# Layer norm 1 of two of four batches on a host-transposed input, in a cross-attention block on one core

## The chip, the core and the metric

The kernel runs on one NeuronCore of a Trainium2 chip. The core has a matrix engine (TensorE, PE in the profile), a vector engine (VectorE, DVE), a scalar engine for activations (ScalarE, ACT), a general engine (GpSimd, POOL) and a sync engine (SyncE, SP) that here issues nearly all DMAs. Each engine works through its own list of instructions in order, and semaphores hold an instruction back until what it needs is there. The metric is the device time of one execution in microseconds, as the median of several runs.

## The reference

Four batches; `hidden_states` x is 4 x 512 x 512, the encoder's states are 4 x 512 x 512, 16 heads of 32, an MLP of 2048, all in float32:

```python
residual = hidden_states
x = layer_norm(hidden_states, ln1_w, ln1_b)
q = (x @ q_w + q_b)          # 16 heads of 32
k = (encoder_hidden_states @ k_w + k_b)
v = (encoder_hidden_states @ v_w + v_b)
scores = jnp.einsum('bhqd,bhkd->bhqk', q, k) * scale
attn = jax.nn.softmax(jnp.where(mask, scores, mask_value), axis=-1)
out = jnp.einsum('bhqk,bhkd->bhqd', attn, v)
hidden = out @ cproj_w + cproj_b + residual
y = layer_norm(hidden, ln2_w, ln2_b)
y = jax.nn.gelu(y @ fc_w + fc_b, approximate=True)
return hidden + y @ proj_w + proj_b
```

Layer norm takes the mean and the variance over the last dimension of each row, subtracts, multiplies by the inverse deviation, and then scales and shifts each column by its weight and bias.

## The kernel before, in words

The attention is done in 16 units, `w` = 0 to 15: unit `w` is batch `b = w // 4` and a group of four heads. For each unit, three preparations run on TensorE ahead of their use: `prep_k` (tile `acck`, L218), `prep_q` (`accq`, L228) and `prep_v` (`accv`, L240). Each is sixteen or four matmuls into one PSUM tile, which ScalarE then empties (L220, L231, L245); GpSimd adds the bias of v (L252). In each unit four query tiles `qt` go through `scores` (TensorE L262, then VectorE adds the mask and finds the minimum, L266, and ScalarE takes the exponential, L270) and `turn` (VectorE transposes 32 x 32 blocks into `tb`, L285 and L293; `rsum` and `rr`, L290 and L292, are the inverse sums). Every two query tiles make one half of a unit, which is rearranged across partitions by 16 DMAs (`copies`, L328, called the exchange) into `pT`, or into parts of `gt` or `xe`. `attend` (L345) then multiplies by v, and VectorE scales into `oT` (L350). There are two buffers of `tb` and one `pT`. Where all four units of a batch are done, `cproj` (L386, L387) projects and adds the residual.

Layer norm 1 of a batch runs some units ahead. `load_x` brings x in four row tiles `xn` (tag of a pool of four buffers), `ln1` takes statistics on VectorE (`ln_stat`, L128 and L129), GpSimd takes the inverse deviation by a power (`ln_rs`, L134 and L136), and `ln_norm` normalises, on VectorE (L150) or, for the keys in `BY_ACT`, on ScalarE (L146, with one more small tile `nm` from GpSimd). `ln_turn` then transposes: for each of four chunks `d`, four 128 x 128 TensorE transpositions (L159) into one PSUM tile `tp`, which is emptied into `xT` with the column's weight and bias, on VectorE for d = 1 and 2 (L162) or on ScalarE (L164). `xT` and the transposed encoder `eT` are two parts of one tile, `xe`; `load_enc` fills `eT` from an array that the host has already transposed. `prep_q` multiplies by `xT`.

Layer norm 2 of a batch goes the same way from `h` into `yT`, with `norm2` and `ln2_turn`. The MLP of batch 0 and part of batch 1's runs between the attention units, in pairs of chunks (`fc_by_pair`, seven products instead of eight, L495, with VectorE's sums L455 and ScalarE's Gelu L513, after a table load), with weight sums on GpSimd (`fc_sums`, L452, L455). The other MLPs come at the end. All accumulations share four PSUM buffers of the pool `ps_acc`, taken in turn.

The order of the work is written out by hand. For each unit `first[w]` and `later[w]` list pieces of work, each a function with a cost. Where `first[w]` is a tuple, its four parts go behind the four query tiles; else the pieces are spread over the four tiles by their costs. A piece issues the instructions of all engines in that order. The pieces `x1`, `x2`, `x3`, `x4` of `inputs(b)` are the load of x, the three parts of `ln1`, the four of `ln1_turn`, and the load of the encoder. DMAs of `nc.sync` go to SyncE's queue in the order of the pieces. `load_w(w + 2)` inside each preparation loads the weights of two units on.

Of the kernel before, what the change touches and what calls it, by code (L numbers as in the profile page):

```python
# [24 lines left out]
NT = L // P  # L25
ND = D // P
# [12 lines left out]
IN_XE = (25, 27, 29, 31)  # L39

AT = {u: (u - 5) // 2 for u in (5, 7, 9, 11, 13, 15, 17, 19, 53, 55, 57, 59, 61, 63)}
BY_ACT = ((1, 1), (1, 2))
MW = 8
WARM = 9
PW = 2 * NT * HG * HD
# [2 lines left out]
LN1W, LN1B, QB, KB, LN2W, LN2B, FCB = 0, 4, 8, 12, 16, 20, 24  # L48
# [1 line left out]


@with_exitstack
def xattn_block(ctx: ExitStack, tc: tile.TileContext, x, encT, mask, q_w, k_w, v_w, c_w, fc_w, p_w, vecs, rows, out):
    nc = tc.nc
    scale = float(np.float32(1.0) / np.sqrt(HD).astype(np.float32))

# [74 lines left out]
    def ln_rs(key):  # L131

        ve = small.tile([P, NT], F32, tag="ve", name=f"ve{key[0]}_{key[1]}")
        nc.gpsimd.tensor_scalar(ve, S["mv", key][:, :, 1], EPS, 1.0, ALU.add, ALU.mult)  # L134
        rs = small.tile([P, NT], F32, tag="rs", name=f"rs{key[0]}_{key[1]}")
        nc.gpsimd.tensor_tensor(rs, ve, nhalf, ALU.pow)  # L136
        S["rs", key] = rs
        if key in BY_ACT:
            nm = small.tile([P, NT], F32, tag="nm", name=f"nm{key[0]}_{key[1]}")
            nc.gpsimd.tensor_tensor(nm, S["mv", key][:, :, 0], rs, ALU.mult)  # L140
            nc.gpsimd.tensor_scalar(nm, nm, -1.0, 0.0, ALU.mult, ALU.add)
            S["nm", key] = nm

    def ln_norm(key, t, dst, src):
        if key in BY_ACT:
            nc.scalar.activation(  # L146
                dst, src, AF.Identity, bias=S["nm", key][:, t : t + 1], scale=S["rs", key][:, t : t + 1]
            )
# [30 lines left out]
    def ln1(b, part):  # L179

        xn = S["xn", b]
        for t in range(NT):
            if part == 2:
                ln_norm((1, b), t, xn[t], xn[t])
            elif t // 2 == part:
                ln_stat((1, b), t, xn[t])
        if part == 1:
            ln_rs((1, b))

    def ln1_turn(b, d):  # L190
        ln_turn((1, b), d, S["xn", b], xT)
# [186 lines left out]
    def c_bias(b):  # L378
        for t in range(NT):
            add_row(S["h", b, t], 0)  # L380
# [339 lines left out]
    def do(fn):  # L720
        return [(0.0, fn)]
# [10 lines left out]
    def C(b):  # L732
        return [(CHAIN, lambda t=t: cproj(b, t)) for t in range(NT)]
# [15 lines left out]
    def inputs(b):  # L749
        ln = [(0.0, lambda part=part: ln1(b, part)) for part in range(3)]  # L750
        return do(lambda: load_x(b)), ln, turns1(b), do(lambda: load_enc(b))
# [55 lines left out]
        [(CHAIN, lambda: prep_q(1))]  # L807
    )
    first[1] = [q2] + x2[2:], [k4], [v4], [q3]
    first[2] = x3[:2] + [k5], x3[2:], [v5], [q4]  # L810
    first[3] = [q5], [k6], [v6], [q6] + do(lambda: c_bias(0))
    mlp = []
    for p in range(SPLIT):
        mlp += FC(p, 0) + FC(p, 1) + PJ(p, 0) + FC(p, 2) + PJ(p, 1) + FC(p, 3) + PJ(p, 2) + PJ(p, 3)
# [25 lines left out]
    def stat(b, *ts_):  # L840
        return do(lambda: [stat2(b, t) for t in ts_])

    def norm(b, *ts_):
        return do(lambda: [norm2(b, t) for t in ts_])


    x1, x2, x3, x4 = inputs(2)
    k, q, v = A(7)
    c, t2 = C(0), turns2(0)
    first[4] = x1 + [k, q, v] + x4  # L850
    later[4] = c[:1] + x2[:1] + c[1:2] + x2[1:2] + c[2:3] + x2[2:] + c[3:]
    k, q, v = A(8)
    first[5] = (
        [k] + stat(0, 0, 1, 2, 3) + rs(0) + do(fc_sums) + x3 + norm(0, 0, 1, 2, 3) + [v], [q] + t2 + do(lambda: y_sums(0)), some(2) + pb_(0), some(2)
    )
    k, q, v = A(9)
    x1, x2, x3, x4 = inputs(3)
    first[6] = [k, q] + some(4) + [v] + x1
    k, q, v = A(10)
    first[7] = [k, q] + x2[:1] + some(2) + x2[1:2] + some(2) + [v]  # L860

    k, q, v = A(11)
    first[8] = h_(1, 0, 1) + x2[2:] + [k, q] + x3[:2] + some(2) + x3[2:3] + [v] + x3[3:] + h_(1, 2, 3) + x4
    later[8] = cb(1) + C(1)
    k, q, v = A(12)
    first[9] = [q] + some(2) + [k] + some(2) + [v]
    k, q, v = A(13)
    first[10] = [k, q] + some(4) + [v]
    k, q, v = A(14)
# [107 lines left out]
```

## Time and profile before

| what | us |
|---|---|
| runs shown: median (lowest to highest) | 803.5 (801.28 to 803.75) |
| profiled execution, its own time | 801.93 |
| profiled execution, span of the profile | 800.2 |
| TensorE matmul records, busy | 785.3 |
| VectorE busy | 573.8 |
| ScalarE busy | 339.5 |
| GpSimd busy | 123.9 |

The profile's records hold for each instruction its start, its length and what ended the idle time before it. The page sums these by group and follows the chain of work that ended last. The records of TensorE are modelled at their ends, so busy TensorE is not TensorE at its peak. In the fences, lines of a timeline read: start, length, engine, line, operation, out<-in, shape, count, and in brackets the idle time before and its releaser. Lines of a group of instructions end in: busy us, mean ns of one, idle before. A DMA line gives KB of each and the median us from issue to landing. A line of windows gives the stretch, its length, the busy time and count of PE, PEld (weight loads), DVE, ACT and POOL, the TensorE clock granted as a share of full speed, the share of the DMA engines that was busy, and GB/s.

The parts of the trace that matter here: unit 4 runs from about 119 to 154 us, unit 5 from 154 to 194, unit 8 from 259 to 300, unit 9 from 300 to 332.

### The profile page before, as it was taken

Reading aid. Unit: us, or ns where it says so; the run is one execution under the profiler, and the core shown is the slowest. Engines: PE = TensorE matmul, PEld = TensorE weight load, DVE = VectorE, ACT = ScalarE, POOL = GpSimd, SP = SyncE. Lnnn points to the kernel's source line nnn. Section 1 sums busy time; section 2 is a strip of 40 time slices with the busy share of each in tenths; the row PEclk is TensorE's granted clock in tenths of the full one; section 3 lists DMA queues with packets and bytes.
Section 4 is the critical chain, followed back from the end, with each engine's and each line's share of the span. In section 5 each row is a group of like instructions: output and inputs, shape, how many; then the busy total and the mean of one; then the engine's idle time right before and its main releaser. Section 6 shows DMA issues by size and latency. Waiting matters only on the chain.

```text
span 800.2 us, 12085 instructions
## 1 busy us (share of the span) xinstructions
PE 785.3 (98%) x4178; PEld 499.4 (62%) x4178; DVE 573.8 (72%) x1179; ACT 339.5 (42%) x745; POOL 123.9 (15%) x146
## 2 busy tenths in 40 slices
PE   9999999989999999999999999999999999999998
PEld 6545455456655645556553433446888888888887
DVE  3789998888888857779878988546738983368511
ACT  2567765547763636456554479500201220022100
POOL 1210030055121141001220100020040020200011
PEclk9999999999999999999999999999999999999999
DMA  8889999847897777787777799882325330033001
GB/s 325 289 230 241 235 237 244 231 115 182 209 240 196 211 210 192 179 198 199 181 173 213 205 261 246 202 254 93 117 84 172 118 106 14 27 86 86 1 14 40
DMA packets 60957, 137.15 MB, mean 171 GB/s; under 512 B 12464, under 2 KB 15664, under 8 KB 60768
## 3 DMA queue, kind: packets, MB, share of 16 engines
q1 hardware_dynamic: 59472, 132.43, 61.3%
q0 software_dynamic: 896, 2.82, 1.1%
q10 hardware_dynamic: 528, 1.14, 0.7%
q8 instruction: 33, 0.54, 0.3%
q14 instruction: 28, 0.23, 0.1%
HBM read 58.22 MB, written 6.82 MB: 81 GB/s over the span
## 4 chain that ended last, share of the span: by engine, by line
PE 87%; DVE 6%; SPq 3%; ACT 1%; issue 1%; DMA 1%; POOL 0%; DVEq 0%; POOLq 0%; ACTq 0%
PE q L495 20%; PE accp L554 8%; PE sc L262 7%; PE accc L386 7%; PE av L345 7%; PE accv L240 6%; PE acck L218 6%; PE accq L228 5%; PE accf L536 3%; DVE ptt L266 3%; SPq L328 2%; PE q4p L622 2%; PE q3p L622 2%; PE q5p L622 2%; PE q6p L622 2%; PE q7p L622 2%
## 5 line engine op out<-in xcount | busy, mean ns | idle before, releaser
L270 ACT ACTIVATE ptt<-ptt,mn 128x512 f32<-128x512 f32 x256 | 181.7, 711 | 135.1 <-DVE mn L266 134.8
L266 DVE CUSTOM_DVE_ANT_0 ptt<-sc,mb 128x512 f32<-128x512 f32 x256 | 161.0, 685 | 32.7 <-PE sc L262 32.4
L285 DVE STREAM_TRANSPOSE tb<-ptt 128x1024 f32<-128x1024 f32 x96 | 119.2, 1242 | 14.4 <-ACT ptt L270 12.9
L554 PE MATMUL accp<-pbt,gt 128*128 128x512 f32 x192 | 86.7, 600 | 0.0
L495 PE MATMUL q<-yT,gt 128*128 128x256 f32 x320 | 78.9, 379 | 0.0
L262 PE MATMUL sc<-pbt 32*128 32x512 f32 x512 | 73.0, 640 | 4.7 <-DVE mn L266 2.5
L513 ACT ACTIVATE ga<-ga,vec 128x512 f32<-128x512 f32 x40 | 26.7, 714 | 93.2 <-DVE ga L455 93.2
L495 PEld LDWEIGHTS q<-yT,gt 128*128 128x128 f32 x320 | 60.8, 190 | 8.7 <-issue 0.5
L554 PEld LDWEIGHTS accp<-pbt,gt 128*128 128x128 f32 x192 | 35.2, 190 | 49.0 <-issue 46.4
L240 PEld LDWEIGHTS accv<-ptt,xe 128*128 128x128 f32 x512 | 58.7, 192 | 9.5 <-issue 6.7
L495 PE MATMUL q<-ys,gt 128*128 128x256 f32 x240 | 61.8, 380 | 0.5 <-DVE ys L452 0.5
L240 PE MATMUL accv<-ptt,xe 128*128 128x128 f32 x512 | 60.8, 277 | 0.0
L218 PE MATMUL acck<-xe,ptt 128*128 128x512 f32 x128 | 59.1, 605 | 0.0
L228 PE MATMUL accq<-xe,ptt 128*128 128x512 f32 x128 | 58.4, 599 | 0.0
L386 PE MATMUL accc<-wc,oT 128*128 128x512 f32 x128 | 56.6, 596 | 0.0
L495 PEld LDWEIGHTS q<-ys,gt 128*128 128x128 f32 x240 | 45.4, 190 | 7.4 <-DVE ys L452 0.9
L345 PE MATMUL av<-pT,v 128*32 128x256 f32 x768 | 48.1, 392 | 1.8 <-DMA gt<-tb 0.7
L498 ACT COPY p<-q 128x256 f32<-128x256 f32 x28 | 9.9, 355 | 92.5 <-PE q L495 92.5
L270 ACT ACTIVATION_READ_ACCUMULATOR ptt<-ptt,mn 128x1 f32 x256 | 47.8, 187 | 0.0
L252 POOL TENSOR_TENSOR v<-v,row 128x512 f32<-128x512 f32 x16 | 20.4, 1275 | 172.9 <-ACT v L245 172.8
L228 PEld LDWEIGHTS accq<-xe,ptt 128*128 128x128 f32 x128 | 23.6, 190 | 32.4 <-issue 30.4
L262 PEld LDWEIGHTS sc<-pbt 32*128 32x128 f32 x512 | 20.0, 182 | 37.9 <-issue 21.4
(137 smaller groups left out, 1071.4 us busy)
## 6 DMA issues: line engine op xcount, KB each, us to landing
pT<-tb SPq DMA_DIRECT2D x384, 136.0 KB, 2.4
pbt<-p_w_dram SPq DMA_DIRECT2D x40, 256.0 KB, 3.1
gt<-fc_w_dram SPq DMA_DIRECT2D x40, 256.0 KB, 2.6
gt<-tb SPq DMA_DIRECT2D x64, 136.0 KB, 3.4
xe<-tb SPq DMA_DIRECT2D x56, 136.0 KB, 3.1
pbt<-fc_w_dram SPq DMA_DIRECT2D x24, 256.0 KB, 3.9
ptt<-k_w_dram SPq DMA_DIRECT2D x16, 256.0 KB, 3.8
xe<-encT_dram SPq DMA_DIRECT2D x16, 256.0 KB, 4.6
```

Of the source, the lines that this page charges most:

```text
L218: nc.tensor.matmul(acc, S["wk", w][:, d, :], eT[:, d, :], start=(d == 0), stop=(d == ND - 1))
L228: nc.tensor.matmul(acc, S["wq", w][:, d, :], xT[:, d, :], start=(d == 0), stop=(d == ND - 1))
L240: nc.tensor.matmul(acc[:, ts(t, P)], eT[:, d, ts(t, P)], S["wv", w][:, d, :], start=(d == 0), stop=(d == ND - 1),)
L262: nc.tensor.matmul(sc[:, h, :], qT[r, ts(qt, P)], kT[r, :], start=True, stop=True)
L266: nc.vector.tensor_tensor_reduce(out=s, in0=sc[:, h, :], in1=S["mb", w // NG], scale=1.0, scalar=FMAX, op0=ALU.add, op1=ALU.min, accum_out=mn,
L270: nc.scalar.activation(s, s, AF.Exp, bias=mn, scale=-1.0, accum_out=sums[:, qt, h : h + 1])
L285: nc.vector.transpose(*two_heads[k])
L345: nc.tensor.matmul(av[ts(h, HD), : 2 * P].rearrange(shape, **kw), v[:, t, ts(h, HD)], p[t][h], start=(t == 0), stop=(t == NT - 1),)
L386: nc.tensor.matmul(acc, S["oT", b][:, g, ts(t, P)], wc[:, g, :], start=(g == 0), stop=(g == NG - 1))
L495: nc.tensor.matmul(o, x[:, k], y[:, k], start=(k == 0), stop=(k == 1))
L554: nc.tensor.matmul(acc, gT[q % 2][:, k, ts(t, P)], S["pw", b, q * FQ + k], start=(k == 0), stop=(k == FQ - 1))
L622: nc.tensor.matmul(o[:, t], a[:, c, ts(t, P)], w[:, c], start=(c == pairs[0]), stop=(c == pairs[-1]))
```

## The change

The host also hands in x transposed (`xT`, in the kernel `xTd`), and batches 2 and 3 (`ROWS`) take layer norm 1 in another way. The row tiles of x are still loaded and the statistics taken from them. `ln1_rows` then makes on GpSimd a small tile `sr` with mean and inverse deviation; `store_rows` writes it to DRAM as two rows of 512; `load_rows` reads each row back, broadcast over 128 partitions, into two buffers of the pool of `xn`. `load_xT` loads the transposed x straight into `xT`; `norm_xT` subtracts and multiplies by the rows on GpSimd, eight passes of 128 x 512; `affine_xT` scales and shifts on ScalarE. The normalisation of row tiles, the transpositions and the emptying of their PSUM tiles fall away for these two batches. Batch 1's layer norm 1 stays as it was; layer norm 2 of batch 0 is now normalised on ScalarE (`NORM_ACT`), with VectorE still emptying two of its four PSUM tiles.

The lists of work change: x of batch 2 is loaded in unit 2 and its statistics are taken in unit 3 (both in unit 4 before), its rows are stored at the end of unit 3; in unit 5 the order becomes k, scale-and-shift, q, v; in unit 9 it becomes k, an MLP pair, scale-and-shift, q (q, pair, k before); in unit 8 the load of weights for v comes ahead of the exchange.

```diff
-BY_ACT = ((1, 1), (1, 2))
+BY_ACT = ((1, 1),)
+NORM_ACT = ((1, 1), (2, 0))
+ROWS = (2, 3)
...
         if part == 1:
-            ln_rs((1, b))
+            ln1_rows(b) if b in ROWS else ln_rs((1, b))
+
+    def ln1_rows(b):
+        mv = S["mv", (1, b)]
+        ve = small.tile([P, NT], F32, tag="ve", name=f"ve1_{b}")
+        nc.gpsimd.tensor_scalar(ve, mv[:, :, 1], EPS, 1.0, ALU.add, ALU.mult)
+        sr = small.tile([P, 2, NT], F32, tag="sr", bufs=1, name=f"sr_{b}")
+        nc.gpsimd.tensor_tensor(sr[:, 1], ve, nhalf, ALU.pow)
+        nc.gpsimd.tensor_scalar(sr[:, 0], mv[:, :, 0], 1.0, 0.0, ALU.mult, ALU.add)
+        S["sr", b] = sr
+
+    def store_rows(b):
+        S["dr", b] = dram.tile([2, L], F32, tag=f"dr{b}", name=f"dr{b}")
+        nc.sync.dma_start(out=S["dr", b].rearrange("s (t p) -> p s t", p=P), in_=S["sr", b])
+
+    def load_rows(b):
+        S["rw", b] = [tiles.tile([P, L], F32, tag="xn", name=f"rw{s}_{b}") for s in range(2)]
+        for s in range(2):
+            nc.sync.dma_start(out=S["rw", b][s], in_=S["dr", b][s : s + 1, :].broadcast_to([P, L]))
+
+    def load_xT(b):
+        for d in range(ND):
+            nc.sync.dma_start(out=xT[:, d, :], in_=xTd[b, ts(d, P), :])
+
+    def norm_xT(b):
+        for d in range(ND):
+            nc.gpsimd.tensor_tensor(xT[:, d, :], xT[:, d, :], S["rw", b][0], ALU.subtract)
+            nc.gpsimd.tensor_tensor(xT[:, d, :], xT[:, d, :], S["rw", b][1], ALU.mult)
+
+    def affine_xT(b):
+        for d in range(ND):
+            wd, bd = (vec[:, i + d : i + d + 1] for i in (LN1W, LN1B))
+            nc.scalar.activation(xT[:, d, :], xT[:, d, :], AF.Identity, bias=bd, scale=wd)
...
-    first[2] = x3[:2] + [k5], x3[2:], [v5], [q4]
-    first[3] = [q5], [k6], [v6], [q6] + do(lambda: c_bias(0))
+    x1, x2 = inputs(2)[:2]
+    first[2] = x3[:2] + [k5], x3[2:], [v5] + x1, [q4]
+    first[3] = [q5], [k6] + x2[:1], [v6] + x2[1:2], [q6] + do(lambda: c_bias(0)) + do(lambda: store_rows(2))
...
-    first[4] = x1 + [k, q, v] + x4
-    later[4] = c[:1] + x2[:1] + c[1:2] + x2[1:2] + c[2:3] + x2[2:] + c[3:]
+    first[4] = do(lambda: load_rows(2)) + [k, q, v] + do(lambda: load_xT(2)) + x4 + do(lambda: norm_xT(2))
+    later[4] = c
     k, q, v = A(8)
     first[5] = (
-        [k] + stat(0, 0, 1, 2, 3) + rs(0) + do(fc_sums) + x3 + norm(0, 0, 1, 2, 3) + [v], [q] + t2 + do(lambda: y_sums(0)), some(2) + pb_(0), some(2)
+        [k] + stat(0, 0, 1, 2, 3) + rs(0) + do(lambda: affine_xT(2)) + [q] + norm(0, 0, 1, 2, 3) + do(fc_sums),
+        [v] + t2 + do(lambda: y_sums(0)), some(2) + pb_(0), some(2)
     )
...
-    first[7] = [k, q] + x2[:1] + some(2) + x2[1:2] + some(2) + [v]
+    first[7] = [k, q] + x2[:1] + some(2) + x2[1:2] + some(2) + do(lambda: store_rows(3)) + [v]
...
-    first[8] = h_(1, 0, 1) + x2[2:] + [k, q] + x3[:2] + some(2) + x3[2:3] + [v] + x3[3:] + h_(1, 2, 3) + x4
-    later[8] = cb(1) + C(1)
+    first[8] = (
+        h_(1, 0, 1) + do(lambda: load_rows(3)) + [k, q] + some(2) + do(lambda: load_xT(3)) + [v] + h_(1, 2, 3) + x4
+    )
+    later[8] = cb(1) + do(lambda: norm_xT(3)) + C(1)
     k, q, v = A(12)
-    first[9] = [q] + some(2) + [k] + some(2) + [v]
+    first[9] = [k] + some(2) + do(lambda: affine_xT(3)) + [q] + some(2) + [v]
...
+        "xT": np.ascontiguousarray(a["x"].transpose(0, 2, 1)),
```

More of the change, by code (lines that the diff above doesn't have):

```diff
@@ L52, in xattn_block @@
 @with_exitstack
-def xattn_block(ctx: ExitStack, tc: tile.TileContext, x, encT, mask, q_w, k_w, v_w, c_w, fc_w, p_w, vecs, rows, out):
+def xattn_block(ctx: ExitStack, tc: tile.TileContext, x, xTd, encT, mask, q_w, k_w, v_w, c_w, fc_w, p_w, vecs, rows, out):
     nc = tc.nc
@@ L137, in ln_rs @@
         S["rs", key] = rs
-        if key in BY_ACT:
+        if key in NORM_ACT:
             nm = small.tile([P, NT], F32, tag="nm", name=f"nm{key[0]}_{key[1]}")
@@ L144, in ln_norm @@
     def ln_norm(key, t, dst, src):
-        if key in BY_ACT:
+        if key in NORM_ACT:
             nc.scalar.activation(
@@ L844, in norm @@
         return do(lambda: [norm2(b, t) for t in ts_])
-    x1, x2, x3, x4 = inputs(2)
+    x4 = inputs(2)[3]
     k, q, v = A(7)
     c, t2 = C(0), turns2(0)
-    first[4] = x1 + [k, q, v] + x4
-    later[4] = c[:1] + x2[:1] + c[1:2] + x2[1:2] + c[2:3] + x2[2:] + c[3:]
+    first[4] = do(lambda: load_rows(2)) + [k, q, v] + do(lambda: load_xT(2)) + x4 + do(lambda: norm_xT(2))
+    later[4] = c
     k, q, v = A(8)
     first[5] = (
-        [k] + stat(0, 0, 1, 2, 3) + rs(0) + do(fc_sums) + x3 + norm(0, 0, 1, 2, 3) + [v], [q] + t2 + do(lambda: y_sums(0)), some(2) + pb_(0), some(2)
+        [k] + stat(0, 0, 1, 2, 3) + rs(0) + do(lambda: affine_xT(2)) + [q] + norm(0, 0, 1, 2, 3) + do(fc_sums),
+        [v] + t2 + do(lambda: y_sums(0)), some(2) + pb_(0), some(2)
     )
     k, q, v = A(9)
-    x1, x2, x3, x4 = inputs(3)
+    x1, x2, _, x4 = inputs(3)
     first[6] = [k, q] + some(4) + [v] + x1
     k, q, v = A(10)
-    first[7] = [k, q] + x2[:1] + some(2) + x2[1:2] + some(2) + [v]
+    first[7] = [k, q] + x2[:1] + some(2) + x2[1:2] + some(2) + do(lambda: store_rows(3)) + [v]
     k, q, v = A(11)
-    first[8] = h_(1, 0, 1) + x2[2:] + [k, q] + x3[:2] + some(2) + x3[2:3] + [v] + x3[3:] + h_(1, 2, 3) + x4
-    later[8] = cb(1) + C(1)
+    first[8] = (
+        h_(1, 0, 1) + do(lambda: load_rows(3)) + [k, q] + some(2) + do(lambda: load_xT(3)) + [v] + h_(1, 2, 3) + x4
+    )
+    later[8] = cb(1) + do(lambda: norm_xT(3)) + C(1)
     k, q, v = A(12)
-    first[9] = [q] + some(2) + [k] + some(2) + [v]
+    first[9] = [k] + some(2) + do(lambda: affine_xT(3)) + [q] + some(2) + [v]
     k, q, v = A(13)
```

## The prediction

> **What bounds the kernel now.** I read the page first: busy times and the chain that ended last.
>
> ```profile
> PE 785.3 (98%) x4178; PEld 499.4 (62%) x4178; DVE 573.8 (72%) x1179; ACT 339.5 (42%) x745; POOL 123.9 (15%) x146
> PE 87%; DVE 6%; SPq 3%; ACT 1%; issue 1%; DMA 1%; POOL 0%; DVEq 0%; POOLq 0%; ACTq 0%
> ```
>
> TensorE carries 87% of the chain and its records leave some 15 us of 800 uncovered. From 192 to 435 us the chain is TensorE alone: there, work taken off it is gained in full, and any wait put in front of it is paid in full. VectorE relief is worth nothing there. Second, the chain in order of time where it leaves TensorE, in unit 5 (the first of the two places the change rewrites), with TensorE's timeline and clock (four lines of the chain: start, length, what; two of the timeline; one window).
>
> ```profile
> 171.64 0.40 ACT rr L292
> 172.04 0.59 ACT pbt L231
> 172.68 0.66 PE tp L159 x4
> 173.35 3.61 PE av L345 x32
> ...
> 168.16 1.47 PE L159 MATMUL tp<-ident,xn 128*128 128x128 f32 x12
> 172.68 0.66 PE L159 MATMUL tp<-ident,xn 128*128 128x128 f32 x4 [3.05 <-ACT pbt L231]
> ...
> 170.00:180.00 10.00, 7.30 (x53) 4.02 (x54) 8.05 (x18) 4.97 (x11) 4.91 (x4) 0.83 0.15 35
> ```
>
> Twelve transpositions of layer norm 2 of batch 0 run; the fourth group waits 3.05 us for a PSUM buffer that ScalarE empties late (L231 stands behind four exponentials, those behind VectorE). Then the clock granted is half for 3.4 us (0.83 over this window, the last column but two), and an L345 group takes 3.61 us for its usual 1.86. So this place costs 3.05 + 1.75 = 4.8 us. Third, the orders of ScalarE and TensorE in unit 9, the second place:
>
> ```profile
> 310.63 1.03 PE L495 MATMUL q<-ys,pbt 128*128 128x256 f32 x4
> 311.50 3.60 PE L218 MATMUL acck<-xe,ptt 128*128 128x512 f32 x8
> 313.62 1.33 ACT L513 ACTIVATE gt<-gt,vec 128x512 f32<-128x512 f32 x2 [2.09 <-DVE gt L455]
> 315.13 0.69 ACT L220 ACTIVATE pbt<-acck,vec 128x512 f32<-128x512 f32 x1 [0.18 <-PE acck L218]
> ```
>
> Now TensorE goes from the products of an MLP pair (L495) straight to `acck`, whose inputs lie ready, while ScalarE's Gelu waits for VectorE's sums until 313.62. Last, SyncE's queue (start, length), then the us to landing of a DMA, then prices of instructions (busy us, mean ns):
>
> ```profile
> 98.31 10.17 SPq L328 DMA_DIRECT2D gt<-tb  x16
> 133.20 1.81 SPq L177 DMA_DIRECT2D xn<-x_dram  x4
> 136.06 12.80 SPq L328 DMA_DIRECT2D pT<-tb  x16
> 149.53 1.87 SPq L172 DMA_DIRECT2D xe<-encT_dram  x4
> ...
> pT<-tb SPq DMA_DIRECT2D x384, 136.0 KB, 2.4
> xe<-encT_dram SPq DMA_DIRECT2D x16, 256.0 KB, 4.6
> vec<-vecs_dram ACTq DMA_DIRECT2D x1, 20.0 KB, 3.9
> ...
> L146 ACT ACTIVATE xn<-xn,nm,rs 128x512 f32<-128x512 f32 x8 | 5.8, 802 | 0.0
> L357 POOL TENSOR_TENSOR h<-h,row 128x512 f32<-128x512 f32 x18 | 22.4, 1276 | 9.8 <-DMA h<-x_dram 5.7 <-PE sc L262 4.1
> ```
>
> SyncE issues without a pause from 95 to 151 us (an exchange is 16 issues at 0.635 us), so what is put into it there moves all behind it.
>
> **Removed.** 32 transpositions on TensorE: 16 a batch, 4 groups of 0.44 us = 1.75 us a batch (the pieces of 0.87, 0.44 and 0.44 us in unit 8). For batch 3 that is a gain of 1.75. For batch 2 the end of unit 5 is set by a wait, so only the replay below counts. VectorE loses the normalisations of batches 0 (L150, 3.5 us) and 3 (1.9) and two L162 (1.6); in unit 8 it is covered by TensorE, worth nothing.
>
> **Moved: statistics and loads of batch 2, from unit 4 to units 2 and 3.** Four pairs of L128 and L129, 0.8 us each, now stand in VectorE's order before the scores of unit 3. By replay its reading of the last scores of unit 3 ends at 120.0 for 117.66, and TensorE's next scores start at 120.0 for 118.77: 1.2 us late. The four loads go ahead of the exchange at 98.31, making SyncE 1.9 us late; its consumer at 112.20 loses about 1 us, part of the same 1.2. Neither adds to the end by itself if unit 5 waits for something later, which it does.
>
> **Added for batch 2, the wait.** SyncE's order is now: store of the rows, two broadcast loads that wait for the store to land, two weight loads, the exchange of unit 4, a weight load, four loads of transposed x, four of the encoder. The store (1,024 pieces of 4 bytes) has no row of its kind. Nearest: 2.4 us to landing for an exchange DMA, 3.9 for the 128 short rows of `vec`. Low end 2.4; high end, if the 1.5 us above 2.4 went by pieces, 2.4 + 8 x 1.5 = 14.4. I take 4, next to `vec`, the only short-row one. Then: store at 135.1, landed 139.2, row loads and weights 2.0, exchange from 141.2 (136.06 before), 10.2 us as it has four loads before it and not seven, x loads from 152.0, the first landed at 155.5 (between 2.4 and 4.6). GpSimd's eight passes at 1.24 (the L357 row's spacing; four took 4.97) end at 165.4. Their cover, the scores and `acck(8)`, ends at about 161.4 as the encoder loads come some 4.4 us later too. From there all is serial: ScalarE's last scale-and-shift 0.8 (L146), the last quarter of `accq(8)` 0.9, its eviction 0.7, four normalisations of batch 0 now on ScalarE 2.9 (four L146 took 2.92), four exponentials 2.9, the reciprocals and `rr` 0.6, `v`'s eviction 0.6, and with it the PSUM buffer for the fourth transposition group: 174.9. One yT eviction 0.8, L345 at full clock 1.9: next scores at 177.6, before at 176.96. Cost +0.7. Queued behind ScalarE's wait are exactly those exponentials, and VectorE's transposes behind them; GpSimd's weight sums (L452, L455, 5.9 us) slide from 164.2 to 167.2, ahead of their use after 178. Floor: if the rows came early, the statistics of batch 0 (end 164.7), GpSimd's 1.9 and ScalarE's 2.9 + 2.9 + 1.2 + 0.8 + 1.9 still give 176.4, so -0.6. Ceiling: each us of the store above 4 is a us, up to +10.4 more.
>
> The Trainium skill ("DMA: Bandwidth & Descriptors", Rules for kernel authors) speaks against the store: a last dimension that isn't contiguous becomes a descriptor for each element. The same page puts about 2 us of fixed cost on a DMA; by that alone the rows land at the floor and the total would be 805.4.
>
> **Added for batch 3, the wait on TensorE.** Loads, rows and GpSimd's passes (297 to 307) are hidden: they are due at 313. `cb(1)`'s loads and the exchange of unit 8 slide 2.5 us (280.5 to 290.7, used at 296); the encoder lands by 298 for 299. But in unit 9 `accq` now follows the MLP products, and its four scale-and-shifts stand on ScalarE behind the Gelu. On the old clock: products end 311.66, Gelu ends 314.95, first scale-and-shift 315.75, `accq` 3.44: 319.2 where `acck` ended at 315.09, so +4.1, less the 1.75 of transpositions: +2.4. The idle of 4.1 us is longer than the 3.05 that halved the clock for 3.4 us above, so I add 1.7 (half of 3.4): +4.1. Bounds 0 and 1.75 for that term.
>
> The Trainium skill ("TensorE: Matmul & The Clock Gate", What's actually happening) lets the clock fall after an idle free-running window of about 3.4 us; a gap of 4.1 need not hold a whole one. By the page the drop is not sure and the total would be 805.0; the row, a gap of 3.05 that did it, decides.
>
> **Sum.** 801.93 (profiled execution; span 800.2) + 0.7 + 4.1 = 806.7. The median of the runs shown is 803.5, by which it is 808.3. I name the middle, 807.5.
>
> **Rivals.** *A, no clock drop* in unit 9: 801.93 + 0.7 + 2.4 = 805.0. For it: gaps of 1.41 and 1.63 us elsewhere dropped nothing; against it: the 3.05. *B, the store is slow* and SyncE stands still: at 9 us to landing +5, 811.7; at 14.4, 817. For it: every us on that queue between 95 and 151 moves the exchange; against: packets of 160 bytes are short in the trace (3.9 us for all). It decides from about 4 us to landing. *C, faster*: the new order dissolves the wait in unit 5, 4.8 us, which needs `v` emptied before 170, so GpSimd done by about 160.5 and the loads landed by 150.5; with A's +2.4 the time is 801.93 - 4.8 + 2.4 = 799.5, and 797 if unit 9's wait half vanishes. For it: VectorE is 3.5 us lighter there; against: the exchange ahead of the loads ended at 148.9 even before, and four normalisations now delay the exponentials. That the transpositions are not removed is excluded: the order of instructions lacks them.
>
> **How the numbers follow.** Forecast 0.50, A 0.19, B 0.17, C 0.14. 0.3% is 2.4 us, about what can be told from no change. Slower: the forecast nearly all, B, and half of A's, as 805.0 lies at the edge: 0.70. Same: the rest of A and some of the forecast, 0.16. Faster: C, 0.14. The range 801.5 to 814 leaves out most of C and the far half of B.
>
> **What would show it.** In the profile after: an idle of about 4 us on TensorE before `accq` in unit 9, ended by ScalarE's scale-and-shift, and a half clock right after; in unit 5 `accq(8)` fed in steps of 2.5 us by GpSimd, L345 back at 1.9 us; the store's time to landing (4 assumed) and SyncE's stop before the row loads; scores of unit 5's third tile about 0.7 us later. Wrong would be: `accq` of unit 9 without an idle, GpSimd's eight passes ending before 160, or GpSimd slowed far above 1.24 us a pass.

## The result and the profile after

The changed kernel takes 825.5 us, median of four runs (822.59 to 828.16), against 803.6 us of the kernel before on the same chip (four runs, 801.28 to 804.95): a ratio of 1.0275, 95% interval 1.0232 to 1.0318. The forecast was 807.5 us, with a range up to 814. The profiled execution took 824.72 us, its span is 822.9.

The page's busy times and the chain that ended last, of the changed kernel:

```profile
PE 787.8 (96%) x4146; PEld 498.6 (61%) x4146; DVE 567.6 (69%) x1169; ACT 341.1 (41%) x747; POOL 144.6 (18%) x164
...
PE 73%; DVE 9%; SPq 8%; DMA 4%; ACT 2%; issue 2%; POOL 1%; DVEq 0%; POOLq 0%; ACTq 0%
```

TensorE's work shrank by 32 matmul records and yet its busy time is 2.5 us longer (its clock is half for 20.5 us, 3.41 before), and it holds 73% of the chain for 87%. SyncE's queue and the DMAs rose from 4% to 12%, VectorE from 6% to 9%. So most of what was lost is in waits for transfers. Where, the starts of the score groups tell (L262 of the kernel before, L296 of this one; lines have moved by 34). The columns after the first are us later than before, from one profiled execution of each kernel; at 50 us, ahead of all that was changed, these are within 0.3 us of each other.

| scores of | before, us | changed kernel | store of 8 rows | no store | early passes | batch 3 alone |
|---|---|---|---|---|---|---|
| unit 4, first tile | 118.70 | +1.46 | +2.71 | +1.86 | +2.21 | -0.85 |
| unit 5, third tile | 176.90 | +10.44 | +3.30 | +0.93 | +4.10 | -1.46 |
| unit 8, first tile | 258.81 | +10.46 | +4.04 | +1.81 | +5.03 | -0.42 |
| unit 9, first tile | 299.58 | +12.90 | +2.29 | +0.06 | +3.28 | -2.17 |
| unit 9, third tile | 316.89 | +20.27 | +8.32 | +6.09 | +3.28 | -2.17 |
| unit 15, last tile | 499.68 | +22.67 | +9.80 | +8.21 | +5.48 | -1.40 |

(The last four columns belong to the experiments.) The 22.7 us of the changed kernel are 1.5 up to unit 4, 9.0 in units 4 and 5, 2.5 in units 6 to 8 (4.2 lost, since 1.75 of transpositions are saved there), 7.4 in unit 9 and 2.4 later.

**Units 4 and 5.** SyncE's queue in the timeline of the changed kernel (start, length, line, what), and its DMAs (KB of each, median us to landing; the store's two took 8.2 and 10.8):

```profile
135.79 0.39 SPq L203 DMA_DIRECT2D dr<-sr  x1
144.05 0.80 SPq L208 DMA_DIRECT2D rw<-dr  x2
...
145.91 14.34 SPq L362 DMA_DIRECT2D pT<-tb  x16
```

```profile
rw<-dr SPq DMA_DIRECT2D x4, 256.0 KB, 6.9
dr<-sr SPq DMA_DIRECT2D x2, 4.0 KB, 9.5
```

The row loads (L208) are issued 8.26 us after the store (L203), because they wait for its landing. That is the wait that was forecast, at twice its length. The second thing to see is the exchange behind (L362): 14.34 us, where 16 issues took 12.80 before with seven loads ahead of it, and 10.2 were forecast. What the DMA engines did meanwhile stands in the last two columns of the windows (their busy share, and GB/s):

```profile
135.00:139.00 4.00, 4.00 (x16) 1.74 (x16) 3.99 (x11) 2.59 (x8) 1.26 (x1) 1.00 0.65 136
139.00:143.00 4.00, 4.00 (x10) 1.52 (x8) 3.11 (x5) 1.26 (x4) 0.00 (x0) 1.00 0.02 4
143.00:147.00 4.00, 4.00 (x43) 1.73 (x43) 1.91 (x5) 0.06 (x1) 0.00 (x0) 1.00 0.00 0
```

From 139 to 147 us the DMA engines move next to nothing. This alone doesn't show whether the store stops them or SyncE has nothing to send. TensorE's timeline shows what comes of it, in units 4 and 5 (first lines), in unit 8, and in unit 9 (last two):

```profile
162.53 3.64 PE L379 MATMUL av<-pT,v 128*32 128x256 f32 x32 [9.34 <-DMA ptt<-v_w_dram]
...
172.74 2.84 PE L262 MATMUL accq<-xe,ptt 128*128 128x512 f32 x6 [1.48 <-ACT xe L222]
...
187.33 1.14 PE L296 MATMUL sc<-pbt 32*128 32x512 f32 x8
...
309.56 2.98 PE L379 MATMUL av<-pT,v 128*32 128x256 f32 x32 [3.05 <-DVE rsum L324]
...
324.12 1.03 PE L529 MATMUL q<-ys,pbt 128*128 128x256 f32 x4
329.20 6.16 PE L262 MATMUL accq<-xe,ptt 128*128 128x512 f32 x8 [4.06 <-ACT xe L222]
```

TensorE stands 9.34 us before `av` (L379), whose `pT` comes from that late exchange (the releaser named is only the DMA behind the exchange in the same queue). The scores of unit 5's third tile start at 187.33 for 176.90. That `av` and what follows it up to 166.9 also run at half clock: `av` takes 3.64 us for 1.93 at full clock.

**Unit 8.** The second store goes out at 267.64, and SyncE needn't wait for it. Still, the exchange behind it takes 14.80 us for 10.03 before (first line, of the kernel before; the others are SyncE's queue and GpSimd's timeline of the changed kernel), the loads that follow it are late, and GpSimd stands in order behind one of them:

```profile
259.65 10.03 SPq L328 DMA_DIRECT2D pT<-tb  x16
...
267.64 0.39 SPq L203 DMA_DIRECT2D dr<-sr  x1
270.10 14.80 SPq L362 DMA_DIRECT2D pT<-tb  x16
...
297.50 0.71 POOL L489 TENSOR_TENSOR wsum<-pbt 128x256 f32<-128x256 f32 x1 [26.83 <-DMA pbt<-fc_w_dram]
...
310.43 2.50 POOL L391 TENSOR_TENSOR h<-h,row 128x512 f32<-128x512 f32 x2 [6.27 <-DMA h<-x_dram]
312.89 1.27 POOL L216 TENSOR_TENSOR xe<-xe,rw 128x512 f32<-128x512 f32 x1
```

Its weight sums (L489) start at 297.50; 277.94 before. Its passes over transposed x, forecast for 297 to 307, run from 312.89 to 323.3; 10.5 us of that delay come from units 4 and 5, 5.4 from here. TensorE loses 3.05 us before `av` at 309.56, and the clock is half for 3.41 us behind that.

**Unit 9.** The idle of 4.06 us before `accq` is there. ScalarE's timeline shows the order that makes it:

```profile
327.11 1.33 ACT L547 ACTIVATE gt<-gt,vec 128x512 f32<-128x512 f32 x2 [2.08 <-DVE gt L489]
328.35 2.91 ACT L222 ACTIVATE xe<-xe,vec 128x512 f32<-128x512 f32 x4
```

The Gelu (L547) waits for VectorE's sums, the scale-and-shift (L222) stands behind it, and `accq` needs the scale-and-shift. The clock is half from 327.36 for 6.83 us, so `accq` takes 6.16 us (3.60 before).

### The profile page after: what moved, and what is told of

Same layout as the page of the kernel before. It is cut to its first block, busy times and chain, and to the rows that moved or that the text cites. A ratio compares the mean times of both kernels' runs of the same rounds, so it can differ in the third digit from the quotient of the medians.

```text
span 822.9 us, 12041 instructions
## 1 busy us (share of the span) xinstructions
PE 787.8 (96%) x4146; PEld 498.6 (61%) x4146; DVE 567.6 (69%) x1169; ACT 341.1 (41%) x747; POOL 144.6 (18%) x164
## 4 chain that ended last, share of the span: by engine, by line
PE 73%; DVE 9%; SPq 8%; DMA 4%; ACT 2%; issue 2%; POOL 1%; DVEq 0%; POOLq 0%; ACTq 0%
PE q L529 18%; SPq L362 8%; PE accp L588 7%; PE av L379 6%; PE sc L296 6%; PE acck L252 5%; PE accq L262 5%; PE accv L274 4%; PE accc L420 4%; DVE ptt L300 4%; PE accf L570 3%; PE q4p L656 2%; PE q3p L656 2%; PE q5p L656 2%; PE q6p L656 2%; PE q2p L656 2%
## 5 line engine op out<-in xcount | busy, mean ns | idle before, releaser
L296 PE MATMUL sc<-pbt 32*128 32x512 f32 x512 | 74.0, 648 | 4.8 <-DVE mn L300 2.5
L262 PE MATMUL accq<-xe,ptt 128*128 128x512 f32 x128 | 61.1, 621 | 5.9 <-ACT xe L222 5.9
L547 ACT ACTIVATE ga<-ga,vec 128x512 f32<-128x512 f32 x40 | 26.7, 714 | 93.2 <-DVE ga L489 93.2
L379 PE MATMUL av<-pT,v 128*32 128x256 f32 x768 | 49.2, 398 | 16.4 <-DMA ptt<-v_w_dram 10.0
L379 PEld LDWEIGHTS av<-pT,v 128*32 128x32 f32 x768 | 24.9, 113 | 41.5 <-issue 22.8
L262 PEld LDWEIGHTS accq<-xe,ptt 128*128 128x128 f32 x128 | 24.4, 197 | 39.8 <-issue 29.4
```

Of the source, the lines that this page charges most:

```text
L262: nc.tensor.matmul(acc, S["wq", w][:, d, :], xT[:, d, :], start=(d == 0), stop=(d == ND - 1))
L296: nc.tensor.matmul(sc[:, h, :], qT[r, ts(qt, P)], kT[r, :], start=True, stop=True)
L379: nc.tensor.matmul(av[ts(h, HD), : 2 * P].rearrange(shape, **kw), v[:, t, ts(h, HD)], p[t][h], start=(t == 0), stop=(t == NT - 1),)
```

## Experiments

Theory S after this reading: the store of 1,024 pieces of 4 bytes holds the whole DMA path, twice. Unit 9's loss is another matter, of order. Rivals: the two broadcast row loads are slow; only SyncE's wait costs; the queue and not the engines is held.

**1. Is it the store, and for whom?** Three kernels. The first writes the rows by 8 pieces of 512 bytes:

```diff
-        nc.sync.dma_start(out=S["dr", b].rearrange("s (t p) -> p s t", p=P), in_=S["sr", b])
+        tr = acc_tile(f"tr_{b}")[: 2 * NT, :P]
+        nc.tensor.transpose(tr, S["sr", b].rearrange("p s t -> p (s t)"), ident)
+        row8 = tiles.tile([P, D], F32, tag="xn", name=f"row8_{b}")[: 2 * NT, :P]
+        nc.vector.tensor_scalar(row8, tr, 1.0, 0.0, ALU.mult, ALU.add)
+        nc.sync.dma_start(out=S["dr", b].rearrange("s (t p) -> (s t) p", p=P), in_=row8)
```

> Mean and deviation are first turned by one TensorE transposition, so that the store writes 8 rows of 512 bytes in place of 1,024 pieces of 4 bytes; all else as in the changed kernel. Theory S (the pieces of the store hold the whole DMA path for some 8 to 10 us each time): the store lands in about 2.5 us, the exchange of unit 4 takes about 10 to 11 us again (14.3 in the changed kernel), the third tile's scores of unit 5 come at about 177.5 to 178.5 (187.3; 176.9 before), unit 8's 3 us go too, and the time is about 813 (825.5 less 9.5 and 3). Rival L (the two broadcast loads, 256 KB each out of one 2 KB row, are what is slow): only the store's own landing shrinks, by some 5 us; the loads keep 6 to 7 us, the exchange stays near 14; about 820. Rival C (an idle TensorE costs more by its clock than by the wait): the time falls by more than the 12.5 us.

Measured: 811.72 us (811.54 to 813.53), ratio to the kernel before 1.0102 (1.008 to 1.0124). 13.8 us are gone. SyncE's row loads go out 2.1 us after the store, the exchange of unit 4 takes 10.73 us, that of unit 7 10.05:

```profile
136.90 0.36 SPq L207 DMA_DIRECT2D dr<-row  x1
139.00 1.75 SPq L212 DMA_DIRECT2D rw<-dr  x2
...
141.81 10.73 SPq L366 DMA_DIRECT2D pT<-tb  x16
...
160.61 4.27 PE L256 MATMUL acck<-xe,ptt 128*128 128x512 f32 x8 [2.01 <-DMA xe<-encT_dram]
```

Third scores of unit 5 are at 180.19, some 2 us later than expected; the last line, of TensorE, is a wait that remains there, for the encoder's loads. Rival C has a part in the gain, as more than 12.5 us went: the half clock fell from 20.5 us to 3.41.

The second leaves the store out, the third keeps it but lets nobody read it:

```diff
-            nc.sync.dma_start(out=S["rw", b][s], in_=S["dr", b][s : s + 1, :].broadcast_to([P, L]))
+            nc.sync.dma_start(out=S["rw", b][s], in_=rows[s : s + 1, :].broadcast_to([P, L]))
```

> The store is left out; the two row loads read two rows of an input of the same size instead (the normalisation takes wrong rows for batches 2 and 3, the work is the same). Theory S: without the store everything that stood behind it moves freely, the row loads land in about 3 us, unit 5's third scores at 176.5 to 178, and the time is about 812 to 813. Rival L: the broadcast loads still take 6 to 7 us and the exchange behind them is as slow as in the changed kernel: 818 to 820.

> The store stays as it is, but nobody reads what it wrote: the row loads read the input rows as in the run without the store, so SyncE waits for nothing. This parts two readings of the store. Theory S (the traffic of the pieces holds the queues behind it, whoever waits): the row loads, the weights and the exchange of unit 4 are still held up, third scores of unit 5 at 183 to 187, and unit 8 loses its 3 us as well: 820 to 825. Rival W (only SyncE's wait for the landing costs, the rest of the queue would run): as without the store, 812 to 814.

Measured: 810.39 without a store (expected 812 to 813), 822.86 with a store that nobody reads. SyncE's queue without the store (its exchange of unit 4):

```profile
138.11 12.34 SPq L361 DMA_DIRECT2D pT<-tb  x16
```

and with the unread store:

```profile
138.28 0.39 SPq L203 DMA_DIRECT2D dr<-sr  x1
138.73 1.05 SPq L208 DMA_DIRECT2D rw<-rows_dram  x2
...
140.83 22.22 SPq L362 DMA_DIRECT2D pT<-tb  x16
```

Here SyncE waits for nothing: the row loads go out 0.45 us after the store. Yet these two land only after 14.5 and 15.3 us (4.6 and 5.5 without the store), and the exchange takes 22.22 us for 12.34. Both rivals fall: the broadcast loads are about as quick as others once the store is gone, and taking SyncE's wait away brings nearly nothing: between unit 4's first scores and unit 5's third this kernel loses 8.3 us, the changed one 9.0, the one without a store gains 0.9. The traffic of the store is what costs, some 9.2 us here. The whole difference to the run without a store, 12.5 us, isn't all the store's: some 3.5 us of it arise ahead of the first store (an idle of 2.63 us before `av` in unit 3 and a half clock after it), so that unit 5's third scores, at 190.6, miss the expected 183 to 187. And the 3 us expected in unit 8 aren't lost: the second store lands after 9.93 us and the exchange behind it takes 13.54, but TensorE has no wait there. What a hold costs depends on what stands behind it.

**2. The queue or the engines?** The unread store is issued by ScalarE, in a queue of its own:

```diff
-        nc.sync.dma_start(out=S["dr", b].rearrange("s (t p) -> p s t", p=P), in_=S["sr", b])
+        nc.scalar.dma_start(out=S["dr", b].rearrange("s (t p) -> p s t", p=P), in_=S["sr", b])
```

> The unread store of 1,024 pieces again (822.9), but issued by ScalarE into its own queue, in which nothing else stands then. Theory Q (the hold is in SyncE's own queue: what stands behind the pieces in it waits): SyncE's row loads, weights and exchange pass by, the time is near the run without a store, 810.4 to 812.5. Theory E (the pieces hold the 16 DMA engines that all queues share): the exchange of unit 4 is as slow as with the store in SyncE's queue, 18 to 22 us, and the time is 819 or more.

Measured: 829.45 us. ScalarE sent the store at 123.88, earlier than SyncE would have, so it met another exchange than the one that the expectation names. SyncE's queue and the windows of this kernel:

```profile
114.41 19.27 SPq L362 DMA_DIRECT2D pT<-tb  x16
```

```profile
126.00:130.00 4.00, 4.00 (x10) 1.73 (x10) 2.53 (x8) 3.16 (x9) 0.62 (x1) 1.00 0.00 0
130.00:134.00 4.00, 1.57 (x4) 0.38 (x2) 0.00 (x0) 1.03 (x2) 0.00 (x0) 1.00 0.48 6
```

An exchange in SyncE's queue was under way and takes 19.27 us, with 0 and 6 GB/s moved between 126 and 134. Fifteen of its sixteen DMAs had gone out and landed as usual (the last of them in 2.5 us); the sixteenth goes out at 133.17, when the store has landed. So SyncE had nothing in flight, and its stop alone doesn't show that transfers under way are held. A load of the mask in GpSimd's queue, issued at 126.26, does (us to landing; the first line is of the kernel before, the second of this run):

```profile
m<-mask_dram POOLq DMA_DIRECT2D x3, 64.0 KB, 4.2
```

```profile
m<-mask_dram POOLq DMA_DIRECT2D x1, 64.0 KB, 11.3
```

So it isn't SyncE's queue: one store of ScalarE's queue holds SyncE's next DMA and a load in GpSimd's. Theory E holds in so far as all queues stand; whether the DMA engines hold, or something behind them, isn't shown (from 126 to 130 their busy share is 0.00).

**3. What of the store?** Seven forms of the unread store, each run once, all with the row loads that read nothing of it. The edits change the DRAM tile's shape and what is written, for instance (32 bytes apart):

```diff
-        S["dr", b] = dram.tile([2, L], F32, tag=f"dr{b}", name=f"dr{b}")
-        nc.sync.dma_start(out=S["dr", b].rearrange("s (t p) -> p s t", p=P), in_=S["sr", b])
+        S["dr", b] = dram.tile([2, L, 8], F32, tag=f"dr{b}", name=f"dr{b}")
+        nc.sync.dma_start(out=S["dr", b].rearrange("s (t p) o -> p s t o", p=P)[:, :, :, 0], in_=S["sr", b])
```

> The unread store of the third run (822.9), but into a DRAM tile of the same layout as its source: 128 pieces of 32 bytes in place of 1,024 of 4, the same 4 KB out of the same 128 partitions. Theory N (it is the number of pieces that holds the path): an eighth of the pieces holds it for about a us, the exchange of unit 4 takes 12 to 13 us again (22.2), the whole is near the run without a store, 810.4 to 812. Rival P (any store that takes small pieces out of 128 partitions to DRAM holds it, the 8-row store was quick for its 8 partitions): the exchange stays near 20 us and the time at 819 or more.

> The unread store by SyncE, of the means alone: 512 pieces of 4 bytes (1,024: 822.9; 128 of 32 bytes: 813.8; none: 810.4). If the hold goes by the number of pieces (theory N: 8.2 to 10.8 us for 1,024, so 4 to 5.5 us for 512, and 3 us to landing for 128 pieces), the first store lands in 5 to 6.5 us, the exchange of unit 4 takes 16 to 18 us (22.2 and 12.3) and the time is 815 to 818. If it is a fixed cost that any store of single elements pays (theory F), it lands in 8 us or more and the time is 820 or more.

> 512 pieces held the path as long as 1,024 (10.3 and 9.9 us to landing), so the number of pieces is not the measure between these. This run keeps the unread store of 1,024 pieces of 4 bytes, but each goes to a place of its own in DRAM, 512 bytes from the next. Theory H (pieces written side by side into the same stretch of DRAM, by different DMA engines, have to wait for each other): the store lands in 3 to 5 us, the exchange of unit 4 takes 12 to 14 us, and the time is 811 to 814 (810.4 without a store). Theory F (a write of 4 bytes is slow wherever it goes): 8 us or more to landing, exchange 18 us or more, 820 or more.

> The unread store of one column alone: 128 pieces of 4 bytes, side by side in 512 bytes of DRAM. The run with 128 pieces of 32 bytes landed in 3.0 us (813.8). Theory H: the neighbours still wait for each other, but if the wait goes by the pieces that share a stretch, it is as long as with 512 and 1,024 pieces, which share as many: 8 us or more, 820 or more. Theory N (it goes by the number of pieces, up to some limit below 512): 3 to 4 us to landing, 811 to 814. Theory F (4 bytes are slow as such): 8 us or more, 820 or more.

> The unread store of 1,024 pieces of 4 bytes, 32 bytes apart in DRAM (4 apart: 9.9 us to landing; 512 apart: 4.0). If the pieces wait for neighbours in the same 32 bytes (as 128 pieces of 32 bytes, side by side, landed in 3.0 us), it lands in 3.5 to 5 us and SyncE's exchange of unit 4 takes 12 to 14 us. If the shared stretch is longer, 64 bytes or more, it still takes 7 us or more and the exchange 17 us or more.

> The same pieces 64 bytes apart. A stretch of 32 or 64 bytes: 3.5 to 5 us to landing, exchange of unit 4 in 12 to 14 us. A longer one: 7 us or more, 17 us or more. No stretch (a slow fall with the distance): between the values of the runs with 32 and 128 bytes.

> The same pieces 128 bytes apart. A stretch of 128 bytes or less: 3.5 to 5 us to landing, exchange of unit 4 in 12 to 14 us; a stretch of 256 or 512 bytes: 7 us or more and 17 us or more.

| the unread store | us to landing, lowest to highest of 2 | exchange of unit 4, us | lost from unit 4's first to unit 5's third scores, us | time, us |
|---|---|---|---|---|
| none | | 12.34 | -0.9 | 810.39 |
| 1,024 x 4 bytes, 4 bytes apart | 9.8 to 9.9 | 22.22 | 8.3 | 822.86 |
| 512 x 4 bytes, 4 apart | 8.8 to 11.8 | 20.30 | 9.3 | 822.94 |
| 128 x 4 bytes, 4 apart | 7.1 to 7.7 | 19.20 | 6.1 | 816.81 |
| 128 x 32 bytes, 32 apart | 2.4 to 3.7 | 12.98 | 0.7 | 813.81 |
| 1,024 x 4 bytes, 32 apart | 3.8 to 4.6 | 13.37 | 1.6 | 812.56 |
| 1,024 x 4 bytes, 64 apart | 3.7 to 4.6 | 13.59 | 0.6 | 811.03 |
| 1,024 x 4 bytes, 128 apart | 3.6 to 4.4 | 13.45 | 3.5 | 813.43 |
| 1,024 x 4 bytes, 512 apart | 3.5 to 4.6 | 13.29 | 2.3 | 816.52 |

The rows come from five chips, on which the kernel before took 803.4 to 804.7 us, and the times hold what else each execution lost; landing and exchange are the measure.

The two lines that decide, from the DMA lists of the run with 128 pieces side by side and of that with 1,024 pieces 32 bytes apart:

```profile
dr<-sr SPq DMA_DIRECT2D x2, 0.5 KB, 7.4
```

```profile
dr<-sr SPq DMA_DIRECT2D x2, 4.0 KB, 4.2
```

An eighth of the pieces, side by side, holds the path nearly as long; 1,024 pieces 32 bytes apart hold it hardly at all, though spaced stores still cost units 4 and 5 some 1.5 to 4.5 us against no store. My first reading, the number of pieces, fell with the 512; a fixed price of any 4-byte piece fell with those 32 bytes and more apart. What counts is the distance in DRAM: pieces 4 bytes apart hold the path, pieces 32 apart don't, and more than 32 brings nothing further (8 and 16 weren't tried). That neighbours within the same 32 bytes wait for each other is an explanation that fits, and so is a limit to the pieces in some longer stretch; no record shows either. Of the expected times, three missed: 128 pieces of 32 bytes took 813.8 for up to 812, with landing and exchange as expected; the run at 512 bytes lost 3.18 us before `av` in unit 3 (0.86 in the run without a store), ahead of any store, and so is at 816.5 for 811 to 814; and 128 pieces cost 816.8 and not 820, landing in 7.1 where 8 or more was expected. Of the 6 us between this run and the one with 1,024 pieces, 5.0 arise ahead of the store.

**4. Unit 9.** On top of the store of 8 rows, the scale-and-shift goes ahead of the MLP pair:

```diff
-    first[9] = [k] + some(2) + do(lambda: affine_xT(3)) + [q] + some(2) + [v]
+    first[9] = [k] + do(lambda: affine_xT(3)) + some(2) + [q] + some(2) + [v]
```

> The store of 8 rows as in the first run of this group, and in unit 9 the scale-and-shift is put ahead of the MLP pair on ScalarE, so that it doesn't stand behind the Gelu. Theory G (unit 9's loss is that order alone: 4.06 us idle and half a clock for 6.83 us): no idle before the q projection of unit 9, clock full from 320 to 340, and the time is 6.8 us (4.06 and half of 6.83, less the 0.7 that the transpositions give) below the first run: about 806. Rival M (the wait only moves: the scale-and-shift now waits for GpSimd's passes with the exponentials or Gelu behind it): the idle shows again before the pair or at the next scores, and less than 3 us are gained.

Measured: 810.67 us (808.77 to 812.1), 1.0 less than the kernel with the 8-row store (811.72), whose runs overlap with these. The expected 806 wasn't reached; rival M was right. GpSimd's timeline, then ScalarE's, then TensorE's of this kernel:

```profile
299.97 2.50 POOL L395 TENSOR_TENSOR h<-h,row 128x512 f32<-128x512 f32 x2 [6.93 <-DMA h<-x_dram]
302.43 1.28 POOL L220 TENSOR_TENSOR xe<-xe,rw 128x512 f32<-128x512 f32 x1
```

```profile
312.85 0.82 ACT L226 ACTIVATE xe<-xe,vec 128x512 f32<-128x512 f32 x1 [1.76 <-POOL xe L221]
```

```profile
317.49 5.40 PE L266 MATMUL accq<-xe,ptt 128*128 128x512 f32 x8 [2.62 <-ACT p L536]
```

GpSimd waits 6.93 us for the residual's load, so its passes begin at 302.43, and the last scale-and-shift can't start before 312.85. Behind it on ScalarE stand the exponentials and the copy of a product (L536), and `accq` now waits for the buffer that this copy frees. The next kernel takes this away: passes ahead of the late residual rows, scale-and-shift at the end of unit 8.

```diff
+        if b == 1 and t >= 2:
+            add_row(h, 0)
         if not stays(b, t):
...
-    later[8] = cb(1) + do(lambda: norm_xT(3)) + C(1)
+    later[8] = do(lambda: [add_row(S["h", 1, t], 0) for t in (0, 1)]) + do(lambda: norm_xT(3)) + C(1) + do(lambda: affine_xT(3))
...
-    first[9] = [k] + some(2) + do(lambda: affine_xT(3)) + [q] + some(2) + [v]
+    first[9] = [k] + some(2) + [q] + some(2) + [v]
```

> The 8-row store (811.7), and for batch 3 GpSimd's passes go ahead of the residual rows that it waits for (the row is added to these behind the projection instead), and the scale-and-shift stands on ScalarE at the end of unit 8. This is what the second try at unit 9 lacked: there GpSimd began its passes at 302.4 because it waited 6.9 us for the residual's load. Theory G (unit 9's loss is only that ScalarE's scale-and-shift comes late, and a half clock after it): passes from about 293 to 303, no idle before the q projection of unit 9, clock full there, and 4.1 + 1.7 = 5.8 us are gained: 805.5 to 806.5. Rival M (the wait moves once more, to the exponentials of unit 9's first tile behind the scale-and-shift): under 3 us gained, 809 or more.

Measured: 806.28 us (802.98 to 807.98), ratio 1.003 (1.0012 to 1.0047). Against the 8-row store 5.4 us are gained of the 5.8 expected (4.6 if each is taken against the kernel before on its own chip). TensorE's timeline, at the same place as above:

```profile
313.91 1.03 PE L535 MATMUL q<-ys,pbt 128*128 128x256 f32 x4
314.78 3.60 PE L266 MATMUL accq<-xe,ptt 128*128 128x512 f32 x8
```

No idle, and 3.60 us as in the kernel before; by the scores all of unit 9's 6.03 us are gone. Unit 9's loss was the late scale-and-shift (behind the Gelu, and without it behind GpSimd's late passes) and the clock after it, theory G.

**5. Can it pay?** Batch 3 alone in the new way (the last run's version), batch 2 as in the kernel before:

```diff
-ROWS = (2, 3)
+ROWS = (3,)
```

> The version of the third run of this group for batch 3 alone; batch 2 takes layer norm 1 as in the kernel before, and units 2 to 5 are as there. If the theory of three places holds (unit 4 to 5 from the store and the late loads, unit 8 from the store, unit 9 from the order on ScalarE), all three are gone, and what is left is the gain of 16 transpositions, 1.75 us, less about 0.7 for the transposition and copy of the rows ahead of unit 8: 802 to 803.5 against 804 before. If batch 3's new way costs something that has not been seen (in unit 8 or later), it is 805 or more.

Measured: 803.17 us (799.98 to 805.0, ten runs) against 803.71, ratio 0.9984 (0.9966 to 1.0002). That can't be told from no change. The scores of unit 9 come 2.17 us earlier in the profiled execution, but 1.46 of these are there in unit 5, ahead of what was changed; 0.7 us go again in unit 12, where `av` waits 0.77 us for `pT`. The last kernel takes both batches in the new way, with unit 9's early passes; for batch 2 the store, the row loads and the loads of transposed x and of the encoder were moved to GpSimd's queue:

```diff
+    def queue_of(b):
+        return nc.gpsimd if b == 2 else nc.sync
...
-    first[4] = do(lambda: load_rows(2)) + [k, q, v] + do(lambda: load_xT(2)) + x4 + do(lambda: norm_xT(2))
-    later[4] = c
+    first[4] = do(lambda: load_rows(2)) + [k, q] + do(lambda: load_xT(2)) + [v] + x4 + do(lambda: norm_xT(2))
+    later[4] = c + do(lambda: affine_xT(2))
```

> A version that could beat both: batch 3 as in the run with GpSimd's early passes (806.3), and for batch 2 the store of 8 rows, the row loads, the loads of transposed x (already behind the q projection of unit 4) and of the encoder are issued by GpSimd into its own queue, so that SyncE has ten DMAs fewer ahead of and behind the exchange of unit 4; the scale-and-shift goes to the end of unit 4. Theory D (what is left of unit 5's loss is that loads and exchange come late out of SyncE's queue): the exchange of unit 4 starts at about 137 (141.8), GpSimd's passes end at about 151 (167.3), no idle before the projections of unit 5, no 3.05 us wait and half clock there either, and third scores of unit 5 at 173 to 175 (180.2 to 181; 176.9 before): 799 to 801. Rival V (unit 5 is set by VectorE's and ScalarE's order: statistics of batch 0, normalisation, exponentials, whatever the loads do): third scores at 176 or later and 803 or more.

Measured: 812.44 us (809.15 to 813.73), ratio 1.0098 (1.0061 to 1.0135): 6 us worse than what it was to better. TensorE's timeline:

```profile
145.95 2.64 PE L386 MATMUL av<-gt,v 128*32 128x256 f32 x32 [2.51 <-DMA gt<-tb]
...
179.15 1.11 PE L161 MATMUL tp<-ident,xn 128*128 128x128 f32 x4 [2.78 <-ACT v L286]
...
183.77 1.52 PE L303 MATMUL sc<-pbt 32*128 32x512 f32 x8
```

GpSimd's passes did end at 150.3, and the projections of unit 5 have no idle. But an exchange of SyncE, from 124.30, took 14.04 us while GpSimd's loads ran beside it, the exchange of unit 4 began no sooner (142.20; 141.81 with the 8-row store in SyncE's queue), and the wait of the fourth transposition group, the one of the kernel before, is back at 2.78 us with a half clock behind it. Early loads alone don't take unit 5's wait away. Theory D falls for the loads; its other half, an earlier exchange, didn't come about here and stays untested.

## Why the prediction was wrong

- **The step that failed is the store's price:** "I take 4, next to `vec`, the only short-row one." It landed in 8.2 and 10.8 us. The row chosen, 128 rows of 160 bytes read from DRAM, has no pieces under 32 bytes; the store packs eight into 32. The bounds of the term reached to 14.4, but rival B priced it as a wait of SyncE alone ("every us on that queue between 95 and 151 moves the exchange").
- **What was missing behind it:** the transfers of all queues stand while such a store is under way. The forecast had the exchange of unit 4 from 141.2 to 151.4; it ran from 145.91 to 160.25, 8.9 us later: 0.7 as the store went out later, 4.1 for the landing, 4.1 for the exchange itself (14.34 for 10.2). Unit 5's third scores were forecast 0.7 us late and came 10.4 late. The first wait was another one, too: `av` for the exchange (9.34 us), where the forecast's chain went through GpSimd's passes and ScalarE.
- **"Loads, rows and GpSimd's passes (297 to 307) are hidden"** fell for the same reason. The second store, which nobody waited for, was priced at nothing; it made the exchange of unit 7 4.8 us longer and, with the delay from unit 5, put the passes at 313 to 323. With the 8-row store the exchange took 10.05 us again and the passes began at 301.9, of which 4.0 are the delay so far.
- **By place:** the profile lost 22.7 us, the forecast had 4.8. Of the 17.9 between them 9.7 are in units 4 and 5, 4.2 in units 6 to 8, 1.6 in unit 9 and 2.4 behind it.
- **Right:** in the run without a store, from the first scores of unit 8 to those of unit 9 1.75 us are gained (1.75), and from there to unit 9's third tile 6.03 are lost (4.1 idle and 1.7 of clock). VectorE's statistics cost unit 3 1.3 us in the changed kernel (1.2), GpSimd's passes are 1.30 us apart (1.24), and rival A is out, the clock did fall.
- **Wrong in unit 5 even with a quick store:** without a store its third scores come 0.93 us late, which is near the 0.7 by luck, as the 0.7 held 4 us for the store and the sum's floor was -0.6. In three kernels with the 8-row store, whose row loads went out after 2.1 to 2.4 us, they come 3.3, 4.4 and 4.1 us late. The term that was too small is the cover: the encoder's loads, to be 4.4 us later than before, landed 7.1 to 8.4 us later in the first of these, and `acck(8)` ended at 164.9 and not at 161.4. ScalarE empties it ahead of its first scale-and-shift, and `accq` then ran without a break, so it was this that it had waited for and not GpSimd.
- **Off in size:** in the changed kernel the half clock of unit 9 lasted 6.83 us and not 3.4, so that unit 9 lost 7.4 us and not the 6.0 of the run without a store.
- **Not foreseen and not settled:** 2.4 us behind unit 9's third tile, 2.1 in the run without a store, in small waits of `av` (0.58, 1.05 and 0.64 us in the changed kernel, two of them for `pT`). No run took them apart.
- **Rival C** ("faster") needed the loads early and unit 5's wait gone. The run with GpSimd's queue had the loads early, and the wait stayed at 2.78 us (3.05).

The Trainium skill ("DMA: Bandwidth & Descriptors", Rules for kernel authors) warned against this store, as a last dimension that isn't contiguous becomes a descriptor for each element. The warning was right, but by the runs the count isn't the price: 1,024 descriptors 32 bytes apart landed in 4.2 us, 128 side by side in 7.4. The same page (Specifications) says that transfers under 512 bytes make the DMA read, modify and write; the runs with pieces 32 bytes apart and more (2.4 to 4.6 us) show no hold that could be put down to it, those 4 bytes apart do; whether it is the cause there no run shows.

## What to carry to other kernels

Before a small tile goes to DRAM one element at a time, transpose it on the chip so that it leaves in whole rows; here that took a matmul of 0.27 us and a copy, and was worth 13.8 us; the new order still cost 1% after it. Price such a store by what it does to every queue, not only by who waits for it. When work is taken off the engine that bounds the time and given to others, follow the receiving engines' own order: here ScalarE's Gelu and GpSimd's wait for a load each cost more than the transpositions did.

## What the hardware showed beside that

The half clock comes in whole steps: 3.41, 6.83 and 10.24 us in these profiles (but for one that the program's end cuts short). This agrees with the free-running window of about 3.4 us of the Trainium skill ("TensorE: Matmul & The Clock Gate", What's actually happening). But no idle of a whole window was needed: in the run with early passes a gap of 1.77 us, with one of 1.60 us that ended 3 us ahead of it, was followed by 3.41 us at half clock, and so were 1.29 and 2.03 us in the run with unit 9's new order, while 1.15 and 2.01 us at the same places in the run with the 8-row store were not. And ten kernels had nearly equal idle times before `accq` of unit 9 (4.01 to 4.07 us): in five of them the clock was half for 3.41 us, in five, the changed one among them, for 6.83. Where it was 6.83, it began inside the idle time (at 327.36 in the changed kernel, idle from 325.14 to 329.20); where 3.41, behind its end (at 319.28 with the 8-row store, idle from 313.95 to 318.02).
